# Layer 3 of a four-layer network: the short convolution moved from TensorE to VectorE and ScalarE, and one more state's product with C moved from VectorE to GpSimd

## The chip, the cores and the metric

The kernel runs on one core of one Trainium2 chip. The metric is device time in microseconds (us): the median of several executions of the whole program, of which layer 3 is the last part. A core has four engines that compute, each with its own queue of instructions, worked off in program order: TensorE (PE, matmuls into PSUM), VectorE (DVE), ScalarE (ACT) and GpSimd (POOL, which here reads and writes SBUF alone). SyncE (SP) issues DMAs. PEld is PE's loading of weights.

## The reference, cut to what matters

Four layers follow one another, each of the form x = x + f(groupnorm(x)), on two images of 192 channels and 96 x 96 positions. Layer 3, the one that the change touches, is a selective scan (a state-space layer) along the 9216 positions of each image:

```python
xz = x_flat @ W_in.T
x_in, z_gate = jnp.split(xz, 2, axis=-1)                  # 384 channels each
...
xc = lax.conv_general_dilated(xt_pad, conv_w, window_strides=(1,), padding='VALID',
                              feature_group_count=D_INNER) + conv_b[None, :, None]
x_conv = jax.nn.silu(xc)                                  # 4 taps per channel
x_dbl = jnp.einsum('bdl,kd->blk', x_conv, W_x)
dt, B_ssm, C_ssm = jnp.split(x_dbl, [DT_RANK, DT_RANK + D_STATE], axis=-1)
...
delta = jax.nn.softplus(dt_lin + b_dt)
def step(h, inp):                                         # 16 states per channel
    dA = jnp.exp(d_t[..., None] * A)
    h = dA * h + (d_t * u_t)[..., None] * B_t[:, None, :]
    y_t = jnp.einsum('bdn,bn->bd', h, C_t)
...
y = ys.transpose(1, 2, 0) + D[None, :, None] * x_conv
y = y * jax.nn.silu(z_gate.transpose(0, 2, 1))
out = jnp.einsum('bdl,cd->bcl', y, W_out)
```

The short convolution is causal: each of the 384 channels is a weighted sum of its value at a position and at the three before it, plus a bias.

## The kernel before, in words

Layer 3 (`layer3`, from L1730) works in 36 steps s: two images b of 18 chunks c, each of T = 512 positions. The 384 inner channels lie as ND = 3 blocks d of 128 partitions, so a full tile is 128 x 1536 in fp32. The state runs over NST = 16 states n, and a state of a chunk goes through this:

- `times_b` (L1902, POOL): bu = du times row n of B. B's row comes as bb, broadcast over the partitions by a DMA from DRAM (`load`, L1894, issued by SP). bu has three buffers, bb four.
- `decay` (L1907, ACT): da = exp(dl times A), into PSUM, one per d, three buffers.
- `scan` (L1916, DVE): h = scan of da and bu, three instructions, one per d. h has three buffers. `keep` (L1922, ACT) saves the last column as the state for the next chunk.
- the product with C. For most states, `spread` (L1926, PE) writes row n of C into PSUM as cc, by a matmul with 16 rows, into a single buffer, and `times_c` (L1937, DVE) forms hc = h times cc, with two buffers. For the states in the tuple `ASIDE` (L1738), C's row comes by DMA as ca, and `times_c` (L1932, POOL) forms hp = h times ca, into a single buffer, one state later.
- `sum_of` (L1945, PE): hc or hp is added into acc in PSUM by six matmul instructions with the identity; for the states in `ASIDE` two states after their product's turn.

Three generators bring the rest of the work, cut at their yields, so that a piece of each falls to each state:

- `output` (from L1957) for the step just ended: y = acc times zs (L1961, DVE), the matmuls with w_out (L1968, PE) and the addition of x (L1976, DVE).
- `late(s+1)` (from L1850), started at n = 3: the matmuls for B, C and dt (L1856), xd and its way to DRAM (br), the matmul for delta (L1871), and softplus: Abs, Relu, Exp, Identity on ACT (L1875 to L1878), at n = 8 a scalar_tensor_tensor on DVE (L1880) and Ln on ACT (L1881), at n = 9 three products on POOL (ln, dl, du: L1883 to L1885).
- `early(s+2)` (from L1800), started at n = 7: the normalised input xn (L1809, ACT), the projection (L1823, PE) in six pieces, copied out of PSUM by ACT to xi (L1831; the three last columns of the chunk before stand in front) and to zs (L1836), then the convolution: four matmuls per d with diagonal matrices, one per tap (L1840), and the bias on ACT on the way to us (L1844); then Silu of zs and us (L1846, L1847).

All three use one PSUM bank, pe, so a piece of PE's waits until the piece before it has been read. The diagonal matrices `taps` are made once (L1778, DVE).

The order on PE, ACT, DVE and POOL is the program's own, written out in the loop at the end of `layer3` (L1995 to L2031): for a state n, `spread`, `scan`, the sums that are due, `times_c` on DVE, `times_b` for two states on, `times_c` on POOL for the state before, the loads for four states on, `decay` for the next state, `keep`, then one piece each of `output`, `late` and `early`. Before the loop, early(0), late(0) and early(1) run through in one go (L1983).

Of the kernel before, what the change touches and what calls it, by code (L numbers as in the profile page):

```python
# [6 lines left out]
F32 = mybir.dt.float32  # L7
I32 = mybir.dt.int32
AF = mybir.ActivationFunctionType
ALU = mybir.AluOpType  # L10
# [8 lines left out]
P = 128  # L19
# [29 lines left out]
ND = DI // P  # L49
# [7 lines left out]
def halves(ap):  # L57

    return ap.rearrange("(k p) t -> p k t", k=2)


class Net:
# [1667 lines left out]
    def layer3(self, x, out, stats):  # L1730


        nc, tc, ins = self.nc, self.tc, self.ins
        T = 512
        NC = HW // T
        NBC = 2 * NST

        ASIDE = (1, 5, 9, 12)  # L1738
        gns = [self.gn(3, b, stats[b]) for b in range(B)]
        with ExitStack() as ctx:  # L1740
            wp = ctx.enter_context(tc.tile_pool(name="w3", bufs=1))
# [8 lines left out]
            cw = self.load("conv_w", [P, ND, 4], pool=wp)  # L1750
            cb = self.load("conv_b", [P, ND], pool=wp)
# [19 lines left out]
            dsk = self.load("D", [P, ND], pool=wp)  # L1771
            w_out = self.load("w_out", [P, ND, C], ins["w_out"].rearrange("(d p) o -> p d o", p=P), wp)

            taps = wp.tile([P, ND, 4, P], F32, name="taps")
            skip = wp.tile([P, ND, P], F32, name="skip")
            for d in range(ND):
                for j in range(4):
                    nc.vector.tensor_scalar(  # L1778
                        taps[:, d, j], self.ident, cw[:, d, j : j + 1], None, ALU.mult
                    )  # L1780
                nc.vector.tensor_scalar(skip[:, d], self.ident, dsk[:, d : d + 1], None, ALU.mult)
            state = wp.tile([P, NST, ND], F32, name="state")
            tail = wp.tile([P, ND, 3], F32, name="tail")
# [13 lines left out]
            def bank():  # L1797
                return ps.tile([P, T], F32, name="pe")

            def early(s):  # L1800


                b, c = steps[s]
                xt = sb.tile([CH, 2, T], F32, name="xt")
                nc.sync.dma_start(out=xt, in_=halves(x[b])[:, :, c * T : (c + 1) * T])
                xn = s1.tile([CH, 2, T], F32, name="xn")
                gs, gb = gns[b]
                for k in range(2):
                    nc.scalar.activation(  # L1809
                        xn[:, k], xt[:, k], AF.Identity, bias=gb[:, k : k + 1], scale=gs[:, k : k + 1]  # L1810
                    )
                us = sb.tile([P, ND, T], F32, name="us")
                zs = s3.tile([P, ND, T], F32, name="zs")
                xi = s1.tile([P, ND, T + 3], F32, name="xi")
                got[s] = {"us": us, "zs": zs}
                if c == 0:
                    nc.gpsimd.memset(tail, 0.0)
                nc.scalar.copy(xi[:, :, 0:3], tail)

                def project(at):  # L1820
                    pe = bank()
                    for k in range(2):
                        nc.tensor.matmul(  # L1823
                            pe, w_in[:, k, at : at + P], xn[:, k], start=k == 0, stop=k == 1
                        )
                    return pe

                for d in range(ND):
                    pe = project(d * P)
                    yield  # L1830
                    nc.scalar.copy(xi[:, d, 3:], pe)  # L1831
                nc.scalar.copy(tail, xi[:, :, T : T + 3])
                for d in range(ND):
                    pe = project(DI + d * P)
                    yield
                    nc.scalar.copy(zs[:, d], pe)  # L1836
                for d in range(ND):
                    pe = bank()
                    for j in range(4):
                        nc.tensor.matmul(  # L1840
                            pe, taps[:, d, j], xi[:, d, j : j + T], start=j == 0, stop=j == 3
                        )
                    yield
                    nc.scalar.activation(us[:, d], pe, AF.Identity, bias=cb[:, d : d + 1])  # L1844
                yield
                nc.scalar.activation(zs, zs, AF.Silu)  # L1846
                nc.scalar.activation(us, us, AF.Silu)  # L1847
                yield
# [39 lines left out]
            def load(s, n):  # L1888

                for name, row in (("bb", NST + n), ("ca", n))[: 1 + (n in ASIDE)]:  # L1890
                    t = sc.tile([P, T], F32, name=name) if name == "bb" else sb.tile(
# [32 lines left out]
            def spread(s, n):  # L1924
                cc = ps.tile([P, T], F32, name="cc")
                nc.tensor.matmul(cc, pick[:, n], got[s]["xd"][:NST], start=True, stop=True)  # L1926
                got[s]["cc", n] = cc

            def times_c(s, n):
                if n in ASIDE:  # L1930
                    hc = s1.tile([P, ND, T], F32, name="hp")
                    nc.gpsimd.tensor_tensor(  # L1932
                        hc, got[s]["h", n], over(got[s]["ca", n]), ALU.mult
                    )
                else:
                    hc = sb.tile([P, ND, T], F32, name="hc")
                    nc.vector.tensor_tensor(  # L1937
                        hc, got[s]["h", n], over(got[s]["cc", n]), ALU.mult
                    )
                got[s]["hc", n] = hc  # L1940

            def sum_of(s, n, last=False):
                hc = got[s]["hc", n]
                for d in range(ND):
                    nc.tensor.matmul(  # L1945
                        got[s]["acc"][:, d], self.ident, hc[:, d], start=False, stop=last
                    )
# [35 lines left out]
            for s, make in ((0, early), (0, late), (1, early)):  # L1983
                for _ in make(s):
                    pass
# [9 lines left out]
            for i, (s, n) in enumerate(chain):  # L1995
                if n == 3 and s + 1 < ns:
                    second = late(s + 1)
                if n == 7 and s + 2 < ns:
                    first = early(s + 2)
                if n not in ASIDE:  # L2000
                    spread(s, n)
# [9 lines left out]
                elif n > 1:  # L2011
                    if n - 1 not in ASIDE:
                        sum_of(s, n - 1)
                    if n - 3 in ASIDE:
                        sum_of(s, n - 3)
                if n not in ASIDE:
                    times_c(s, n)
# [110 lines left out]
```

## Time and profile before

| what | us |
|---|---|
| median of 3 runs | 11979.33 (11973.39 to 11980.73) |
| the profiled execution, its time | 11969.94 |
| the profiled execution, its span | 11968.2 |
| busy over the span: PE | 10378.3 (87%) |
| busy over the span: DVE | 8759.4 (73%) |
| busy over the span: POOL | 6998.9 (58%) |
| busy over the span: ACT | 6054.2 (51%) |
| mean granted clock of TensorE | 0.903 |

The profile is of one execution, and its lines name the engine, the line of the kernel, the operation, and output<-inputs by the program's names. "hc<-h,cc 128x1536 f32 x432 | 757.4, 1753 | 606.7 <-PE cc L1926 593.8" would be read: 432 instructions, 757.4 us busy in all, 1753 ns each on the average, and 606.7 us in which the engine stood idle just before them, of which 593.8 ended when PE had finished cc. In a timeline a line has its start and its length in us, and behind "x1" the idle time before it and what ended that. A matmul in fp32 shows as two instructions. The granted clock is the share of TensorE's clock that the chip let through.

### The profile page before, as it was taken

The numbers are of one execution on the slowest core, as the hardware profiler recorded it, in microseconds if no ns is written. First come the engines' busy times: TensorE is split into PE (matmuls) and PEld (weight loads), VectorE is DVE, ScalarE is ACT, GpSimd is POOL, SyncE is SP. The second block draws the span as 40 slices with busy tenths as digits, with TensorE's granted clock in tenths as the row PEclk, the third lists the DMA queues.
The fourth block names the chain that finished last, engine by engine and source line by source line (L and its number), as shares of the span: only waits on it lengthen the run. The fifth ranks groups of instructions, "written<-read, shape, count | busy, mean of one in ns | idle before, by whom it ended". The sixth has DMA issues, their size and how long they took to land. (4 is left out here: it accounts for less than half of the span.)

```text
span 11968.2 us, 226348 instructions
## 1 busy us (share of the span) xinstructions
PE 10378.3 (87%) x90181; PEld 6063.1 (51%) x90181; DVE 8759.4 (73%) x8880; ACT 6054.2 (51%) x11181; POOL 6998.9 (58%) x5569
## 2 busy tenths in 40 slices
PE   3599999999899999986767777769999999999998
PEld 2488888887788888872212222223333333333333
DVE  3777777776777777765688877747777777777778
ACT  0366666665666666750006533335555555555554
POOL 0366766765666666651036533327677767776777
PEclk9899999999999999998867777769899989988998
DMA  4534444433333333334323211112221222222121
GB/s 107 93 94 94 98 96 95 99 94 78 75 91 91 90 92 92 90 76 140 111 86 98 77 44 49 46 40 60 58 62 57 61 59 61 57 62 60 60 57 52
DMA packets 625509, 928.58 MB, mean 78 GB/s; under 512 B 240064, under 2 KB 325372, under 8 KB 623424
## 3 DMA queue, kind: packets, MB, share of 16 engines
q1 hardware_dynamic: 402248, 713.07, 22.4%
q0 software_dynamic: 103808, 133.18, 5.2%
q10 hardware_dynamic: 118392, 67.73, 1.9%
q8 instruction: 720, 11.80, 0.4%
q14 instruction: 341, 2.79, 0.1%
HBM read 475.14 MB, written 188.78 MB: 55 GB/s over the span
## 5 line engine op out<-in xcount | busy, mean ns | idle before, releaser
L1902 POOL TENSOR_TENSOR bu<-du,bb 128x1536 f32<-128x1536 f32 x576 | 1973.6, 3437 | 841.3 <-issue 538.0
L555 DVE TENSOR_TENSOR sp<-h 128x2304 f32<-128x2304 f32 x790 | 2168.0, 2776 | 20.5 <-ACT h L534 20.5
L1916 DVE TENSOR_TENSOR_SCAN h<-da,state,bu 128x512 f32<-128x512 f32 x1632 | 1962.8, 1263 | 67.3 <-ACT da L1907 45.9
L1907 ACT ACTIVATE da<-dl,sb_A_log 128x512 f32<-128x512 f32 x1728 | 1170.2, 689 | 1485.5 <-DVE h L1916 1479.7
L579 ACT COPY st<-pt 128x512 f32<-128x512 f32 (+1 forms) x2370 | 1219.0, 517 | 1308.7 <-PE pt L571 1239.7
L571 PE MATMUL pt<-ident,sp 128*128 128x128 f32 x14220 | 1680.0, 276 | 125.9 <-DVE sp L555 79.3
L577 DVE COPY st<-pt 128x512 f32<-128x512 f32 x1580 | 1061.3, 686 | 975.8 <-PE pt L571 959.8
L525 POOL TENSOR_TENSOR h<-u,step 128x1152 f32<-128x1152 f32 (+1 forms) x474 | 1201.4, 2547 | 816.6 <-DVE u L498 472.4
L571 PEld LDWEIGHTS pt<-ident,sp 128*128 128x128 f32 x14220 | 1566.7, 142 | 213.3 <-issue 90.1
L543 POOL DMA_DIRECT2D xw<-xp_d x2500 | 1391.7, 633 | 178.8 <-PE pt L618 82.6
L1945 PE MATMUL acc<-hc,ident 128*128 128x512 f32 x2592 | 1366.7, 668 | 8.5 <-DVE hc L1937 8.5
L1937 DVE TENSOR_TENSOR hc<-h,cc 128x1536 f32<-128x1536 f32 x432 | 757.4, 1753 | 606.7 <-PE cc L1926 593.8
L618 PE MATMUL pt<-st,xw 64*32 64x288 f32 (+1 forms) x30000 | 1070.9, 365 | 72.7 <-ACT st L579 27.9
L639 ACT COPY val<-pt 128x288 f32<-128x288 f32 (+1 forms) x3132 | 985.8, 398 | 205.2 <-PE pt L618 201.9
L686 PE MATMUL pf<-main,wd 126*64 126x128 f32 (+1 forms) x17064 | 962.1, 270 | 1.1 <-DMA main<-val 0.4
L686 PE MATMUL pf<-more,wl 54*64 54x128 f32 (+1 forms) x17064 | 953.2, 268 | 10.2 <-DMA more<-val 10.2
L686 PEld LDWEIGHTS pf<-main,wd 126*64 126x64 f32 x17064 | 889.6, 137 | 140.8 <-issue 138.5
L1945 PEld LDWEIGHTS acc<-hc,ident 128*128 128x128 f32 x2592 | 520.8, 212 | 857.3 <-issue 845.9
L686 PEld LDWEIGHTS pf<-more,wl 54*64 54x64 f32 x17064 | 916.1, 135 | 45.7 <-issue 32.0
L618 PEld LDWEIGHTS pt<-st,xw 64*32 64x32 f32 x30000 | 539.0, 106 | 477.0 <-ACT val L639 171.7
L1823 PE MATMUL pe<-xn,sb_w_in 96*128 96x512 f32 x864 | 499.2, 707 | 137.2 <-ACT xn L1809 91.4
L1926 PE MATMUL cc<-xd,pick 16*128 16x512 f32 x864 | 554.5, 725 | 23.0 <-DVE hc L1937 22.9
(317 smaller groups left out, 13751.3 us busy)
## 6 DMA issues: line engine op xcount, KB each, us to landing
main<-val SPq DMA_DIRECT2D x2016, 81.0 KB
bb<-br SPq DMA_DIRECT2D x576, 256.0 KB
more<-val SPq DMA_DIRECT2D x1728, 40.5 KB
xw<-xp_d POOLq DMA_DIRECT2D x2500, 26.0 KB
xt<-x_d SPq DMA_DIRECT2D x108, 384.0 KB
ca<-br SPq DMA_DIRECT2D x144, 256.0 KB
u_d<-u SPq DMA_DIRECT2D x158, 180.0 KB
raw<-o_d SPq DMA_DIRECT2D x156, 180.0 KB
```

The costliest lines, as they stand in the source:

```text
L525: nc.gpsimd.tensor_tensor(hs, u[:, :, 8 * KK * l : 8 * KK * l + n].unsqueeze(3).to_broadcast([P, 2, n, WS]), con["step"].unsqueeze(1).unsq ...
L543: nc.gpsimd.dma_start(out=xw[e * WN : (e + 1) * WN, i], in_=xp_d[y : y + WS, x : x + WS, e * CM // 2 : e * CM // 2 + XW],)
L555: nc.vector.tensor_tensor(sp.rearrange("p s (y x) -> p s y x", x=WS), hy.unsqueeze(3).to_broadcast([P, n, WS, WS]), hx.unsqueeze(2).to_bro ...
L571: nc.tensor.transpose(pt[:, q], sp[:, 2 * (q0 + q) : 2 * (q0 + q) + 2].rearrange("p e w -> p (e w)"), self.ident,)
L577: nc.vector.tensor_copy(st[:, q0 : q0 + m], pt[:, :m])
L579: nc.scalar.copy(st[:, q0 : q0 + m], pt[:, :m])
L618: nc.tensor.matmul(pvs[e][lane : lane + 32, j * w : (j + 1) * w], xw[e * WN : (e + 1) * WN, win, g * CG : g * CG + 32], sts[pair][e * WN : ...
L686: nc.tensor.matmul(to, wt[:, m * CO : (m + 1) * CO], took.rearrange("p h (r c) -> p h r c", c=columns), start=first and l == 0 and t == 0, ...
L1902: nc.gpsimd.tensor_tensor(bu, got[s]["du"], over(got[s]["bb", n]), ALU.mult)
L1907: nc.scalar.activation(da, got[s]["dl"][:, d], AF.Exp, scale=nA[:, d, n : n + 1])
L1916: nc.vector.tensor_tensor_scan(h[:, d], got[s]["da", n, d], bu[:, d], init, ALU.mult, ALU.add)
L1945: nc.tensor.matmul(got[s]["acc"][:, d], self.ident, hc[:, d], start=False, stop=last)
```

## The change

The convolution leaves PE. Its first tap becomes an ACT instruction that reads xi and writes us, with the tap's weight as scale and the bias; the other three become scalar_tensor_tensor instructions on DVE, us = xi times weight + us, in place, nine per step, issued next to the projection of zs. The matmuls with the diagonal matrices, their three yields, the bias on the way out of PSUM and the making of the matrices go. `early` has three pieces fewer, so Silu comes at an earlier state. And `ASIDE` has five states instead of four, three of them other ones.

```diff
-        ASIDE = (1, 5, 9, 12)
+        ASIDE = (1, 4, 7, 10, 12)
...
-            taps = wp.tile([P, ND, 4, P], F32, name="taps")
             skip = wp.tile([P, ND, P], F32, name="skip")
             for d in range(ND):
-                for j in range(4):
-                    nc.vector.tensor_scalar(
-                        taps[:, d, j], self.ident, cw[:, d, j : j + 1], None, ALU.mult
-                    )
                 nc.vector.tensor_scalar(skip[:, d], self.ident, dsk[:, d : d + 1], None, ALU.mult)
...
                     nc.scalar.copy(xi[:, d, 3:], pe)
+                    nc.scalar.activation(
+                        us[:, d], xi[:, d, :T], AF.Identity, bias=cb[:, d : d + 1], scale=cw[:, d, 0:1]
+                    )
                 nc.scalar.copy(tail, xi[:, :, T : T + 3])
                 for d in range(ND):
                     pe = project(DI + d * P)
+                    for j in range(1, 4):
+                        nc.vector.scalar_tensor_tensor(
+                            us[:, d], xi[:, d, j : j + T], cw[:, d, j : j + 1], us[:, d], ALU.mult, ALU.add
+                        )
                     yield
                     nc.scalar.copy(zs[:, d], pe)
-                for d in range(ND):
-                    pe = bank()
-                    for j in range(4):
-                        nc.tensor.matmul(
-                            pe, taps[:, d, j], xi[:, d, j : j + T], start=j == 0, stop=j == 3
-                        )
-                    yield
-                    nc.scalar.activation(us[:, d], pe, AF.Identity, bias=cb[:, d : d + 1])
                 yield
                 nc.scalar.activation(zs, zs, AF.Silu)
                 nc.scalar.activation(us, us, AF.Silu)
```

## The prediction

> **What bounds the kernel now.** I read the page, then parts of layer 3 alone: its waits, the timelines of DVE, POOL, PE and ACT over one step, and the granted clock by stretch. Layer 3 runs from about 8010 us to the end, in 36 steps. Its y (L1961), once in a step, in DVE's timeline (start, us, engine, line, wait before):
>
> ```profile
> 11662.24 1.76 DVE L1961 TENSOR_TENSOR y<-acc,zs 128x1536 f32<-128x1536 f32 x1 [7.30 <-PE acc L1945]
> 11771.46 1.76 DVE L1961 TENSOR_TENSOR y<-acc,zs 128x1536 f32<-128x1536 f32 x1 [7.31 <-PE acc L1945]
> 11869.93 1.76 DVE L1961 TENSOR_TENSOR y<-acc,zs 128x1536 f32<-128x1536 f32 x1 [3.44 <-PE acc L1945]
> ```
>
> A step takes 109.2 us; the third row ends a step without early. In one step (10121.8 to 10231.1) PE is busy 101.3, DVE 82.5, POOL 78.8, ACT 57.1. What DVE waits for between 8200 and 11800: us in all, times, longest:
>
> ```profile
> DVE hc L1937 <- PE cc L1926: 569.3, 264, 6.2
> DVE y L1961 <- PE acc L1945: 241.3, 33, 7.5
> ```
>
> So a step is 84.4 us of DVE's own (start to start: 16 triples of scans at 3.73, 12 hc at 1.67, y 1.68, L1880 1.67, two L1976 at 0.65) and about 25 us of waits, nearly all for PE. Three groups tell what is traded:
>
> ```profile
> L1902 POOL TENSOR_TENSOR bu<-du,bb 128x1536 f32<-128x1536 f32 x576 | 1973.6, 3437 | 841.3 <-issue 538.0
> L1916 DVE TENSOR_TENSOR_SCAN h<-da,state,bu 128x512 f32<-128x512 f32 x1632 | 1962.8, 1263 | 67.3 <-ACT da L1907 45.9
> L1937 DVE TENSOR_TENSOR hc<-h,cc 128x1536 f32<-128x1536 f32 x432 | 757.4, 1753 | 606.7 <-PE cc L1926 593.8
> ```
>
> The scans and hc have one input in PSUM (da, cc), and keep these times beside POOL. A DVE operation with both inputs in SBUF does not. Layer 1, DVE's timeline, then POOL's:
>
> ```profile
> 5959.47 1.74 DVE L1440 TENSOR_TENSOR t<-t,lr 96x1536 f32<-96x1536 f32 x1
> 5961.13 4.99 DVE L1434 TENSOR_TENSOR lr<-pad 96x1536 f32<-96x1536 f32 x1
> ```
>
> ```profile
> 5959.63 4.88 POOL L1431 TENSOR_TENSOR ud<-pad 96x1536 f32<-96x1536 f32 x1 [0.99 <-DVE pad L114]
> ```
>
> POOL issued while L1440 (both inputs in SBUF) ran; it took 4.88 instead of its shortest 3.45 and ended at 5964.51. L1434 issued as L1440 ended, but POOL was already waiting and went first; L1434 ended at 5966.12, one duration behind POOL. They exclude each other, and who waits goes next. In layer 3 it happens once, to the only such DVE operation there now (median 1.751):
>
> ```profile
> 11820.65 3.41 DVE L1880 SCALAR_TENSOR_TENSOR du<-ln,du 128x1536 f32<-128x1536 f32 x1
> ```
>
> ```profile
> 11819.00 3.44 POOL L1902 TENSOR_TENSOR bu<-du,bb 128x1536 f32<-128x1536 f32 x1 [1.96 <-issue]
> ```
>
> L1880 ends 1.62 us behind that product. The new taps read xi and us, both in SBUF.
>
> The clock in two stretches (length; PE, PEld, DVE, ACT, POOL busy; granted clock; DMA):
>
> ```profile
> 10060.00:10070.00 10.00, 8.76 (x12) 2.49 (x10) 9.35 (x8) 6.42 (x10) 8.18 (x3) 0.66 0.22 60
> 10070.00:10080.00 10.00, 8.69 (x10) 3.11 (x11) 3.80 (x3) 5.27 (x9) 3.43 (x1) 0.57 0.30 92
> ```
>
> Half clock follows thin work (matmuls of 16 and 44 rows) or a wait of 2 us, though PE is mostly busy.
>
> **The change, part by part (per step).**
> 1. PE loses the taps, three groups of eight L1840 at 3.55 us = 10.65, and one cc, 1.06: 11.7.
> 2. ACT loses three L1844 (0.68) and gains three scaled copies from SBUF; nearest row L1809, 0.80. They stand behind xi copies, and scan 10 needs the decays behind them only 5 us later: 0; without that cover 2.4.
> 3. DVE loses one hc (1.67) and gains nine scalar_tensor_tensor of 128x512. Nearest rows: L1687, the same operation, 0.67; L1719, with a pointer scalar, 0.74; start to start 0.61 to 0.67. I take 0.61, as for L1682 and L1683 back to back: 5.5 (at most 6.0). DVE's own work: 84.4 - 1.7 + 5.5 = 88.2.
> 4. POOL gains one hp, 24 operations at 3.4 = 81.6. Its ca goes through SP, which waits only for buffers: 0.
> 5. The generator is three yields shorter: Silu moves from n=1 to n=14, with the same two table loads. Scan 3 waited 0.8 for it; at n=14 an hc stands in between: 0 to -0.8, I take 0.
> 6. At the start, early(0) and early(1) run alone: 7967.74 to 7983.34 and 8037.85 to 8054.23 go, 32 us once. Their taps end while z is projected. The twelve L1778 (2.4 us) end before xi is there: 0.
>
> **The walk.** I followed the four queues through one step in program order with these durations; t=0 is the start of scan 0.
> - *y*: PE has no taps before the sum of state 15. The wait falls from 7.3 to the 3.4 of the third y row.
> - *n=1 to 7*: hc3 at 23.6 waits 1.8, hc5 at 36.4 waits 2.9 (before: 1.2, and hc6 2.5). Scan 7 ends at 47.
> - *hc8*: xn waits for ACT's Abs, Relu, Exp and Identity behind scan 7, then projection 0 (3.7 at half clock) and cc8 (2.07) pass on PE. Before: 11.4 from the end of scan 7 to hc8. The same now, but state 7 has no hc to fill it: DVE waits 7.7, not 6.
> - *hc9*: state 9 now has an hc. Its cc stands behind projection 1, which waits for the xi copy behind Ln (t=64). PE has no sums left for that gap and is at half clock: 3.7 + 2.07, hc9 at 69.9, a wait of 4.2 (before: hc10, 3.7).
>
> Waits: 3.4 + 1.8 + 2.9 + 7.7 + 4.2 = 20.0; without exclusion a step is 88.2 + 20.0 = 108.2. PE's relief of 11.7 buys little, since it was late for y alone; its other waits hang on chains through ACT. A check: the step between the second and third y row lacks all of early, 21.8 us of PE's work, and is only 10.7 shorter.
> - *The taps* stand at the ends of n=10, 11, 12, where POOL is fullest: ln, dl and du begin at 63.5 behind Ln, then bu12, bu13, hp10, bu14, bu15, hp12. Behind scan 10: tap, bu13 (3.4), tap, hp10 (3.4), tap: 6.8, and 2.0 more if bu12 still runs. Behind hc11 half of bu14 is left, 1.8, and bu15 isn't free before scan 12. Behind scan 12: tap, bu15, tap, hp12, tap: 6.9. Sum 15.5 (17.5 with bu12). The next scan is queued behind each waiting tap, and ACT's decays, PE's sums and POOL's next bu wait for that scan: nothing catches up. hp10 and hp12 share one buffer and each need a sum of PE first, which comes within 1 us of the turn; a late one drops its 3.4. I take one of two: 12.1.
>
> Step: 108.2 + 12.1 = 120.3, +11.1. Bounds of the exclusion: 0, if no tap meets a product, and 17.5. 34 of 36 steps have an early: 34 x 11.1 = 377, less 32: +345. The profiled execution (span 11968.2) took 11969.94, so 12315; the median of the runs is 9.4 above it, so 12325.
>
> **Two rules of the Trainium skill.** "GPSIMD Engine Reference", 1. Specifications, names "contention with DVE instructions in a 2-port perf mode or with two SBUF inputs". It speaks against this change and gives no price; the rows above show a whole turn waited. "TensorE: Matmul & The Clock Gate", Part 1, has PE throttled after an idle window of about 3.4 us; the first clock row differs, 0.66 with 8.76 of 10 us busy. By the page projection 0 and cc8 keep the full clock after a wait of 2 us, an estimate of 2.9 us less per step, 12226 in all; by the rows 12325.
>
> **Rivals.**
> - *The port does not bite* (faster): the taps slip between products. For it: only one of 36 L1880 was held. Against: L1880 comes while POOL waits for Ln, the taps while POOL is backed up. Step 108.2: 34 x -1.0 - 32 = -66, 11913. It decides if the waits for POOL sum to under 1.9 us per step.
> - *PE's relief passes whole* (faster): 109.2 - 11.7 = 97.5: 34 x -11.7 - 32 = -430, 11549. Against: the check above.
> - *A colder PE* (slower still): while DVE waits for POOL, PE idles, and sums 11 and 13 and a cc at half clock come into DVE's way: 2 x 2.66 + 1.06 = 6.4 more, 126.7: 34 x 17.5 - 32 = +563, 12542.
> - *Less exclusion* (slower, by less): both hp late, 116.9, and full clock through n=8, 114.0: 34 x 4.8 - 32 = +131, 12110.
>
> **Chances.** Forecast (116.9 to 125.7 a step: 12209 to 12508) 0.60; less exclusion 0.12; colder PE 0.10; within 0.2%, about what a measurement here can tell from no change, 0.05; the port does not bite 0.10; whole relief 0.03. So faster 0.13, same 0.05, slower 0.82. The range 12000 to 12560 holds the forecast, the lesser exclusion and most of the colder case.
>
> **What would show it.** Right: taps with a mean above 1.5 us, those of n=10 and 12 the longest; POOL's products above 3.44 in turn; y's wait about 3, hc9's about 4; steps of 120. Wrong: a tap mean near 0.7, or steps at or under 109, or the full clock through n=8.

## The result, and the profile after

The changed kernel takes 12298.48 us (median of 4 runs, 12292.43 to 12331.58) against 11976.36 (4 runs, 11968.79 to 11980.73) for the kernel before on the same chip: a ratio of 1.0271, 95% interval 1.0259 to 1.0282, or +322 us. The forecast was 12325, or +345.

The profiled execution of the changed kernel took 12331.58, its span 12329.5. Layer 3 sets in 33 us later in it than before (its L1767 starts at 7976.50 instead of 7943.19); that time arises in layers that the change does not touch, so the two traces are compared from there: 4353.0 us to the end instead of 4025.0, +328. Mean granted clock 0.877 instead of 0.903.

The taps as a group of the trace from 8000 us to the end (line, engine, operation, tiles; count; busy us, mean ns; idle before). They take nearly three times what such an instruction takes beside no product of POOL's (0.74, below):

```profile
L1834 DVE SCALAR_TENSOR_TENSOR us<-xi,sb_conv_w,us 128x512 f32<-128x512 f32 x315 | 679.1, 2156 | 15.0 <-ACT us L1827 7.6
```

What DVE waits for between 8200 and 11800, as shown for the kernel before (us, times, longest). This stretch holds 30 steps, and 33 of the kernel before. The wait of y has fallen from 7.3 a step to 1.8; that of hc has hardly changed, 17.0 a step (509.6 over 30) instead of 17.3 (569.3 over 33), but it lies at other states:

```profile
DVE hc L1931 <- PE cc L1920: 509.6, 151, 7.9
DVE y L1955 <- PE acc L1939: 53.7, 30, 4.8
DVE hc L1931 <- DVE h L1910: 1.4, 3, 0.5
```

One step on DVE, from hc8 to y (start, length, line; in brackets the wait). The three groups of taps stand behind scan 10, hc11 and scan 12:

```profile
10143.44 1.75 DVE L1931 TENSOR_TENSOR hc<-h,cc 128x1536 f32<-128x1536 f32 x1 [5.20 <-PE cc L1920]
10145.11 2.92 DVE L1874 SCALAR_TENSOR_TENSOR du<-ln,du 128x1536 f32<-128x1536 f32 x1
...
10155.89 1.75 DVE L1931 TENSOR_TENSOR hc<-h,cc 128x1536 f32<-128x1536 f32 x1 [4.32 <-PE cc L1920]
...
10161.11 10.58 DVE L1834 SCALAR_TENSOR_TENSOR us<-xi,sb_conv_w,us 128x512 f32<-128x512 f32 x3
...
10175.33 1.75 DVE L1931 TENSOR_TENSOR hc<-h,cc 128x1536 f32<-128x1536 f32 x1
10177.00 3.86 DVE L1834 SCALAR_TENSOR_TENSOR us<-xi,sb_conv_w,us 128x512 f32<-128x512 f32 x3
...
10184.33 5.34 DVE L1834 SCALAR_TENSOR_TENSOR us<-xi,sb_conv_w,us 128x512 f32<-128x512 f32 x3
...
10210.86 1.76 DVE L1955 TENSOR_TENSOR y<-acc,zs 128x1536 f32<-128x1536 f32 x1 [1.62 <-PE acc L1939]
```

POOL over the same stretch. The 10.58 lie beside bu12, bu13 and hp10: POOL's products and the taps end one after the other, in turn. In the second group only the first tap meets a product (bu14, until 10178.73); the two behind it, just as much in place, take 0.75 each. The last product of the fence, hp12, came only at 10195.03, when the third group was done, so that group met one product and not two:

```profile
10160.03 7.28 POOL L1896 TENSOR_TENSOR bu<-du,bb 128x1536 f32<-128x1536 f32 x2
10167.68 3.45 POOL L1926 TENSOR_TENSOR hp<-h,ca 128x1536 f32<-128x1536 f32 x1 [0.38 <-PE acc L1939]
10175.30 3.43 POOL L1896 TENSOR_TENSOR bu<-du,bb 128x1536 f32<-128x1536 f32 x1 [4.17 <-DVE h L1910]
10184.54 3.79 POOL L1896 TENSOR_TENSOR bu<-du,bb 128x1536 f32<-128x1536 f32 x1 [5.80 <-issue]
10195.03 3.44 POOL L1926 TENSOR_TENSOR hp<-h,ca 128x1536 f32<-128x1536 f32 x1 [6.70 <-issue]
```

From y to y a step takes 118.6 and 120.4 us in turn; the mean of the first 30 is 119.7, before 109.2.

### The profile page after: what moved, and what is told of

Its sections match the earlier page's. It is cut to its first block, busy times and chain, and to the rows that moved or that the text cites. A ratio compares the mean times of both kernels' runs of the same rounds, so it can differ in the third digit from the quotient of the medians.

```text
span 12329.5 us, 224855 instructions
## 1 busy us (share of the span) xinstructions
PE 10204.4 (83%) x89245; PEld 5965.6 (48%) x89245; DVE 9385.8 (76%) x9156; ACT 6075.8 (49%) x11181; POOL 7160.1 (58%) x5605
## 3 DMA queue, kind: packets, MB, share of 16 engines
q14 instruction: 343, 2.81, 0.1%
## 5 line engine op out<-in xcount | busy, mean ns | idle before, releaser
L1896 POOL TENSOR_TENSOR bu<-du,bb 128x1536 f32<-128x1536 f32 x576 | 2003.0, 3485 | 863.0 <-issue 433.9
L1939 PE MATMUL acc<-hc,ident 128*128 128x512 f32 x2376 | 1329.4, 704 | 10.7 <-DVE hc L1931 10.7
L1931 DVE TENSOR_TENSOR hc<-h,cc 128x1536 f32<-128x1536 f32 x396 | 694.4, 1754 | 609.5 <-PE cc L1920 589.0
L1818 PE MATMUL pe<-xn,sb_w_in 96*128 96x512 f32 x864 | 598.9, 830 | 569.8 <-ACT zs L1838 284.0
L686 PE MATMUL pf<-more,wl 54*64 54x128 f32 (+1 forms) x17064 | 957.2, 268 | 11.7 <-DMA more<-val 10.2
L1926 POOL TENSOR_TENSOR hp<-h,ca 128x1536 f32<-128x1536 f32 x180 | 624.7, 3470 | 257.2 <-issue 246.2
```

The costliest lines, as they stand in the source:

```text
L686: nc.tensor.matmul(to, wt[:, m * CO : (m + 1) * CO], took.rearrange("p h (r c) -> p h r c", c=columns), start=first and l == 0 and t == 0, ...
L1896: nc.gpsimd.tensor_tensor(bu, got[s]["du"], over(got[s]["bb", n]), ALU.mult)
L1939: nc.tensor.matmul(got[s]["acc"][:, d], self.ident, hc[:, d], start=False, stop=last)
```

## The experiments

Theory at the outset: the taps read SBUF twice and wait for POOL's products, whole turns at a time; that is the loss, since DVE is what a step hangs on. Rivals: the loss comes from the other choice of states, or from a PE that is late in new places.

All runs in one table. "Waits" are what DVE waited for cc and acc of PE, per step (30 steps from the first y on, from the profiled execution); "the rest" is the step less these waits, that is DVE's own work, the taps, their waits for POOL and what DVE waits for ACT's da and POOL's hp (1.9 before, none in the changed kernel). The ratios are to the kernel before as it ran beside each: 11976.36 for the changed kernel, 11980.84 for the next four rows, 11983.24 for the next four (five_with_9 to taps_psum_old_states), 11983.83 for the last four.

| kernel | median us | ratio to before (95%) | step | waits | rest |
|---|---|---|---|---|---|
| before | 11976.36 | 1 | 109.2 | 24.6 | 84.6 |
| after | 12298.48 | 1.0271 (1.0259-1.0282) | 119.7 | 18.7 | 100.9 |
| one_sbuf_input | 12066.25 | 1.0066 (1.0049-1.0083) | 112.7 | 24.4 | 88.3 |
| no_dve_taps | 11888.45 | 0.9923 (0.9907-0.9940) | 107.7 | 26.0 | 81.7 |
| conv_alone | 12439.37 | 1.0391 (1.0373-1.0408) | 123.8 | 16.8 | 107.1 |
| aside_alone | 12258.21 | 1.0232 (1.0215-1.0249) | 117.4 | 35.5 | 81.9 |
| five_with_9 | 12046.53 | 1.0060 (1.0044-1.0077) | 111.4 | 27.5 | 83.9 |
| one_sbuf_old_states | 11881.33 | 0.9919 (0.9902-0.9936) | 107.0 | 16.2 | 90.8 |
| relief_old_states | 11712.88 | 0.9778 (0.9761-0.9794) | 102.3 | 17.6 | 84.7 |
| taps_psum_old_states | 11872.81 | 0.9914 (0.9897-0.9930) | 106.4 | 14.8 | 91.6 |
| taps_psum_new_states | 11990.16 | 1.0009 (0.9998-1.0021) | 110.5 | 21.6 | 88.9 |
| taps_psum_five_with_9 | 11968.56 | 0.9985 (0.9972-0.9997) | 109.2 | 19.0 | 90.2 |
| after_with_9 | 12474.29 | 1.0416 (1.0393-1.0438) | 124.6 | 19.5 | 105.1 |
| taps_later | 12345.60 | 1.0301 (1.0279-1.0323) | 121.1 | 26.7 | 94.4 |

### The exclusion taken away

one_sbuf_input: the taps' second input is a decay tile in PSUM, so that no tap reads SBUF twice; the sum over the taps is left out by this. (18 of the 324 taps run before the first decay and keep us.)

```diff
-                            us[:, d], xi[:, d, j : j + T], cw[:, d, j : j + 1], us[:, d], ALU.mult, ALU.add
+                            us[:, d], xi[:, d, j : j + T], cw[:, d, j : j + 1],
+                            got["da"] if "da" in got else us[:, d], ALU.mult, ALU.add
...
                 got[s]["da", n, d] = da
+                if d == 0:
+                    got["da"] = da
```

> The nine taps of DVE keep their number, shape and place, but their second input is da, in PSUM, in place of us, so only one input is in SBUF; the sum over the taps is left out by this (us holds the last tap plus a da). Theory (a DVE operation with two SBUF inputs and a POOL product exclude each other): the taps fall from a mean of 2.16 us to 0.7, a step from 118.6 to about 104.4 (14.2 less), in all about 11816, below the kernel before. Rival (the taps cost what they cost as DVE work in a chain, whatever memory they read): taps stay above 1.5 us and the time between 12250 and 12330.

Measured 12066. The taps, from its groups of instructions:

```profile
L1834 DVE SCALAR_TENSOR_TENSOR us<-xi,sb_conv_w,da 128x512 f32<-128x512 f32 x306 | 226.9, 742 | 7.2
```

0.742 us instead of 2.156: the taps' waits for POOL are gone. The rest of a step falls by 100.9 - 88.3 = 12.6. The nine taps give back 12.8 of DVE's time; the scalar_tensor_tensor on du (L1874 in the changed kernel), which still reads SBUF twice, takes 2.81 on the average instead of 2.31, so this kernel is not wholly free of the exclusion. But a step falls by only 7.0, because the waits for PE rise by 5.7. Its DVE timeline shows where, at hc11, hc13 and hc14, none of which waits in the changed kernel:

```profile
10037.32 1.76 DVE L1934 TENSOR_TENSOR hc<-h,cc 128x1536 f32<-128x1536 f32 x1 [3.52 <-PE cc L1923]
10052.05 1.75 DVE L1934 TENSOR_TENSOR hc<-h,cc 128x1536 f32<-128x1536 f32 x1 [1.45 <-PE cc L1923]
10058.69 1.75 DVE L1934 TENSOR_TENSOR hc<-h,cc 128x1536 f32<-128x1536 f32 x1 [1.34 <-PE cc L1923]
```

So the exclusion holds, and my price for taking it away (11816) does not. In the changed kernel the taps' waits lie over a lateness of PE. The stretch table of the changed kernel (length; PE, PEld, DVE, ACT, POOL busy; clock; DMA) has the first group, 10042.43 to 10052.99, in it:

```profile
10040.00:10050.00 10.00, 10.00 (x24) 4.16 (x22) 9.93 (x6) 3.68 (x7) 10.00 (x4) 0.97 0.14 34
10050.00:10060.00 10.00, 3.38 (x6) 1.35 (x6) 9.90 (x6) 2.67 (x5) 5.83 (x2) 0.71 0.16 45
```

While DVE stands in the taps, PE works without a gap on what it owes, at clock 0.97: sums 9 and 7, projections 2 and 3, and cc11, done at 10051.3.

no_dve_taps: the nine taps on DVE are left out altogether.

```diff
-                    for j in range(1, 4):
-                        nc.vector.scalar_tensor_tensor(
-                            us[:, d], xi[:, d, j : j + T], cw[:, d, j : j + 1], us[:, d], ALU.mult, ALU.add
-                        )
```

> Taps 1 to 3 are left out: us is the first tap of ACT with the bias. It shows what is left of a step without any tap on DVE or PE. Theory: a step loses the 19.8 us that the three groups take, 98.8, in all about 11625; if another wait takes part of the room, 100 to 103, up to 11770. Rival (PE's relief was worth 11.7 a step by itself, the taps ate it): 97.5 a step, 11580. The distance to the run with one SBUF input is the taps' own work: 5.5 us a step, 190 in all, by the theory; some 20 us a step by the rival that prices them as DVE work.

Measured 11888. With no tap anywhere, and PE relieved of 11.7 us a step, a step is 107.7. What PE gave up comes back as waits for it (26.0, more than the 24.6 before the change); hc11 waits 6.00 and 5.21 in two successive steps. That the relief passes whole is refuted.

### The two halves alone

conv_alone is the changed kernel with the old states; aside_alone is the kernel before with the new ones.

```diff
-        ASIDE = (1, 4, 7, 10, 12)
+        ASIDE = (1, 5, 9, 12)
```

> The convolution as in the changed kernel, but the states by POOL as before (1, 5, 9, 12). Theory: the exclusion does it, so this is slower than before as well: one hc more on DVE (1.7), one product less on POOL, the taps behind hc10 and hc11 meet half a product each and more of the backlog behind ln: 113 to 119 a step, 12100 to 12310. Rival (the other choice of states does it, with hc9's wait and the empty slot on PE): 103 to 108 a step, under 11940.

```diff
-        ASIDE = (1, 5, 9, 12)
+        ASIDE = (1, 4, 7, 10, 12)
```

> The convolution on PE as before, the five states on POOL as in the change. Theory: DVE has one hc less, PE one cc less, POOL one product more; PE is late for y as before: 107 to 111 a step, 11900 to 12030, within 0.5% of before. Rival (the choice of states does it): 115 or more a step, over 12150.

Measured 12439 and 12258. The convolution alone costs +458 (against 11981 for the kernel before, run beside them), more than both together; the states alone +277, where I had expected a slight change: there my reading of the states fell, and the rival was right. Together they cost +322, not 735. (conv_alone lies 129 above what I had expected of it; why, the runs of the exclusion with the old states show.) In aside_alone the rest of a step is 2.7 shorter than before (one hc of 1.7 and 1.1 less of waits for da and hp make most of it), and the waits for PE are 10.9 longer. DVE's timeline there:

```profile
10009.98 1.75 DVE L1937 TENSOR_TENSOR hc<-h,cc 128x1536 f32<-128x1536 f32 x1 [7.85 <-PE cc L1926]
10021.26 1.75 DVE L1937 TENSOR_TENSOR hc<-h,cc 128x1536 f32<-128x1536 f32 x1 [4.32 <-PE cc L1926]
10035.50 1.75 DVE L1937 TENSOR_TENSOR hc<-h,cc 128x1536 f32<-128x1536 f32 x1 [5.41 <-PE cc L1926]
...
10072.36 1.76 DVE L1961 TENSOR_TENSOR y<-acc,zs 128x1536 f32<-128x1536 f32 x1 [7.31 <-PE acc L1945]
```

hc8 and hc11 now follow states without an hc, so DVE arrives earlier and waits; state 9 has an hc now, whose cc stands behind projection 1. PE, which still has the convolution, is no earlier. five_with_9 puts state 9 aside again, and keeps five:

```diff
-        ASIDE = (1, 5, 9, 12)
+        ASIDE = (1, 4, 6, 9, 12)
```

> The kernel before with five states by POOL, but 1, 4, 6, 9, 12: state 9 stays without an hc. With the five of the change (1, 4, 7, 10, 12) and the convolution on PE a step took about 116.5 instead of 109.2. Theory (it is the place: hc9 needs a cc that stands behind the projection which waits for the xi copy behind Ln, and PE then has no sums to do and goes to half clock): with state 9 free of cc the loss is gone, 107.5 to 110 a step, 11915 to 12010. Rival (it is the number: a fifth product on POOL delays bu and hp): 114 or more a step, over 12150.

Measured 12047, above what I expected by 37. So of the 277 it matters for 212 which the five states are (7 and 10, or 6 and 9); what is left, +66, goes with a fifth state on POOL, and with 4 and 6 in the place of 5. One cost of these states is L1880, the scalar_tensor_tensor on du, which reads SBUF twice: it takes 1.80 on the average before, 2.33 in aside_alone and 3.50 in five_with_9, because POOL is then at a product when it comes:

```profile
10004.34 3.23 DVE L1880 SCALAR_TENSOR_TENSOR du<-ln,du 128x1536 f32<-128x1536 f32 x1
```

```profile
10002.52 3.43 POOL L1902 TENSOR_TENSOR bu<-du,bb 128x1536 f32<-128x1536 f32 x1
```

The +1.7 a step in five_with_9 is not far below the 2.2 that its step is longer than before; but hc10 waits 7.2 for PE behind it, which can hide it, and no run shows what it is worth.

### The exclusion with the old states

The edits of one_sbuf_input and no_dve_taps, with the old states.

> The taps on DVE with one input in SBUF (da from PSUM in place of us; the sum over the taps is left out), and the states by POOL as before (1, 5, 9, 12). With both inputs in SBUF this choice of states took 124 a step, 23.3 of it in the taps. Theory: exclusion is 17.7 of the 23.3, less what PE takes of the room: 107 to 112 a step, 11900 to 12070. Rival (with these states the taps wait for something else): over 118 a step, 12280.

> Taps 1 to 3 are left out, and the states by POOL as before: PE's relief of the convolution alone. Theory (PE was late for y alone, the other waits hang on chains through ACT): y's wait falls from 7.3 to 2 or 3 and little else: 103.5 to 105.5 a step, 11740 to 11820. Rival (the relief passes whole): 98.6 a step, 11585.

Measured 11881 and 11713, 19 and 27 below what the theory gave. Against conv_alone the exclusion costs 558 us with these states, 123.8 - 107.0 = 16.8 a step; seen from DVE it is 107.06 - 90.84 = 16.2 and the waits for PE stay nearly as they are (16.8 and 16.2). Here next to nothing is hidden. The difference lies ahead of the taps. conv_alone on DVE, from hc10:

```profile
10075.32 1.75 DVE L1931 TENSOR_TENSOR hc<-h,cc 128x1536 f32<-128x1536 f32 x1 [2.39 <-PE cc L1920]
10076.99 11.01 DVE L1834 SCALAR_TENSOR_TENSOR us<-xi,sb_conv_w,us 128x512 f32<-128x512 f32 x3
...
10093.32 3.86 DVE L1834 SCALAR_TENSOR_TENSOR us<-xi,sb_conv_w,us 128x512 f32<-128x512 f32 x3
...
10100.64 8.39 DVE L1834 SCALAR_TENSOR_TENSOR us<-xi,sb_conv_w,us 128x512 f32<-128x512 f32 x3
```

State 10 has an hc there, which first waits for PE; then the taps wait for POOL; the two waits stand one behind the other. With the new states the taps come before the next hc that needs PE, and one wait runs inside the other. The third group is also longer here, 8.39, since hp12 isn't late. relief_old_states bears out that PE was late for y above all: without taps on either engine a step is 6.9 shorter than before, the waits for y fall from 7.3 to 1.6, and those for hc by 1.2.

### Is it the hiding? State 9 put aside, and the taps moved

after_with_9 is the changed kernel with states that are better by 212 where the convolution is on PE, and in which state 10 has an hc in front of the taps.

```diff
-        ASIDE = (1, 4, 7, 10, 12)
+        ASIDE = (1, 4, 6, 9, 12)
```

> The changed kernel with the states (1, 4, 6, 9, 12), its taps reading SBUF twice. Theory: the exclusion and the lateness of PE at hc9 and hc11 hide one another; with state 9 aside there is less lateness to hide it, so the exclusion costs nearly its whole (12 to 16 us per step, as with the old states): 12300 to 12450, steps of 119 to 124, not faster than the changed kernel's 12298 although its states are the better ones by 212 without the taps on DVE. Rival, that the two add up: 12298 - 212, so 12050 to 12130, steps of about 113.

taps_later moves the taps away from POOL's fullest stretch.

```diff
                     pe = project(DI + d * P)
+                    yield
+                    nc.scalar.copy(zs[:, d], pe)
+                for d in range(ND):
                     for j in range(1, 4):
...
                     yield
-                    nc.scalar.copy(zs[:, d], pe)
```

> The changed kernel with its nine taps moved behind the projection of z, from n = 10 to 12 to n = 13 to 15; they still read SBUF twice. Theory: a group waits for the products that POOL has in its queue just there; behind n = 12 only one bu per state and one hp are left, so each group meets one product instead of up to two: groups of about 5.5 + 5.5 + 3.9 = 15 instead of 19.8, and a step of 112 to 117: 12040 to 12220. Rival, that the place does not matter because each tap waits for a product wherever it stands: 12250 to 12350.

after_with_9 came to 12474: the better states make the changed kernel slower by 176 us. This is the direction that the hiding foresaw, 24 us beyond its upper end; that the parts add up (12050 to 12130) is refuted. No run takes the exclusion away with these states and the taps in this place, so its price here is not measured by itself. Its DVE timeline has the wait for PE in front of the group, as in conv_alone:

```profile
10093.65 1.75 DVE L1931 TENSOR_TENSOR hc<-h,cc 128x1536 f32<-128x1536 f32 x1 [5.93 <-PE cc L1920]
10095.33 9.12 DVE L1834 SCALAR_TENSOR_TENSOR us<-xi,sb_conv_w,us 128x512 f32<-128x512 f32 x3
```

taps_later came to 12346, and my theory's time (12040 to 12220) fell, though the groups did what it said: 2.32 + 8.06 + 3.91 = 14.3 us, expected 15. The rest of a step fell by 6.5, and the waits for PE rose by 8.0:

```profile
10038.56 1.75 DVE L1933 TENSOR_TENSOR hc<-h,cc 128x1536 f32<-128x1536 f32 x1 [4.32 <-PE cc L1922]
...
10053.33 1.75 DVE L1933 TENSOR_TENSOR hc<-h,cc 128x1536 f32<-128x1536 f32 x1 [5.95 <-PE cc L1922]
...
10065.56 1.75 DVE L1933 TENSOR_TENSOR hc<-h,cc 128x1536 f32<-128x1536 f32 x1 [3.41 <-PE cc L1922]
10067.24 2.32 DVE L1837 SCALAR_TENSOR_TENSOR us<-xi,sb_conv_w,us 128x512 f32<-128x512 f32 x3
```

Between hc9 and hc11 DVE has nothing but scans now, and waits 5.95 for cc11; the taps then stand where PE is not late. The rival's number was right for another reason than it gave: a tap does meet fewer products at the later place, but at the earlier place some 6 us of the wait were free. (This reading came after the run; no forecast of it was made.)

### The sum over the taps in PSUM

Here the convolution is whole: the first tap goes to the PSUM bank that the projections use, the next two add to it there, and the last writes us, in three pieces behind the projection of z. No tap reads SBUF twice; the scalar_tensor_tensor on du still does.

```diff
-                    nc.scalar.activation(
-                        us[:, d], xi[:, d, :T], AF.Identity, bias=cb[:, d : d + 1], scale=cw[:, d, 0:1]
-                    )
                 nc.scalar.copy(tail, xi[:, :, T : T + 3])
                 for d in range(ND):
                     pe = project(DI + d * P)
+                    yield
+                    nc.scalar.copy(zs[:, d], pe)
+                for d in range(ND):
+                    pe = bank()
+                    nc.scalar.activation(
+                        pe, xi[:, d, :T], AF.Identity, bias=cb[:, d : d + 1], scale=cw[:, d, 0:1]
+                    )
+                    yield
                     for j in range(1, 4):
                         nc.vector.scalar_tensor_tensor(
-                            us[:, d], xi[:, d, j : j + T], cw[:, d, j : j + 1], us[:, d], ALU.mult, ALU.add
-                        )
-                    yield
-                    nc.scalar.copy(zs[:, d], pe)
+                            us[:, d] if j == 3 else pe, xi[:, d, j : j + T], cw[:, d, j : j + 1], pe,
+                            ALU.mult, ALU.add,
+                        )
```

With the old states, the changed kernel's, and (1, 4, 6, 9, 12):

> The whole convolution, on ACT and DVE, with its sum held in the PSUM bank pe between the taps, so that every tap has one input in SBUF and one in PSUM; in three pieces behind the z projections (n = 13 to 15, and DVE's last at n = 0), states by POOL as before. Theory (exclusion): taps at 0.75 each, 6.7 a step beside 104.5 without them, DVE has some slack there: 105 to 111 a step, 11800 to 12030. Rival (the taps' place on DVE ahead of the scans costs, whatever they read): 115 or more, over 12180.

> The whole convolution with the sum over the taps held in a PSUM bank, in three pieces behind the projection of z, with the states of the changed kernel (1, 4, 7, 10, 12). Theory: with the exclusion gone, what is left of the slowdown is the choice of states, as in the run with one SBUF input at 12066; the three later pieces changed that by -9 with the old states (11881 to 11873). So 12000 to 12120, steps of 111 to 114, taps of about 0.74 us. Rival, that the states cost by themselves what they cost with the convolution on PE (+277 on 11873): 12120 to 12180.

> The same with the states (1, 4, 6, 9, 12): five aside, state 9 among them. Theory: the states' loss is the place of hc9, whose cc stands behind projection 1; with it gone, 212 as between the two runs with the convolution on PE (12258 to 12047), or somewhat less because PE has room now: 11850 to 11950. Rival, that hc9's place matters only while PE has the taps: within 60 of the run with the changed kernel's states, 12000 to 12120.

With the old states it takes 11873, 0.9% less than the kernel before and 3.5% less than the changed one. A tap takes 0.75, as in the groups of that run:

```profile
L1839 DVE SCALAR_TENSOR_TENSOR pe<-xi,sb_conv_w,pe 128x512 f32<-128x512 f32 x216 | 162.7, 753 | 62.1 <-ACT pe L1834 58.3
```

With the changed kernel's states 11990, 10 below the range that I gave, and no different from before (0.9998 to 1.0021). With state 9 put aside as well 11969, where I had expected 11850 to 11950: 22 us better and not some 200, so the place of hc9 is worth little once PE has no taps, as the rival had it, whose range it misses by 31. Four states beat five wherever no tap reads SBUF twice: on PE (11976 and 12047 or 12258), with one SBUF input (11881 and 12066), without taps (11713 and 11888) and in PSUM. Part of it can be du's turn with POOL, whose operation takes 1.80 with the old states, 2.55 with the changed kernel's and 3.25 with the last; this is not shown by itself.

## Why the prediction was right

The sum came out within 27 us. Taken term by term it describes the changed kernel for the reasons given; but the prediction built it as a step without exclusion, 108.2, and a price of exclusion on top, 12.1, and there the runs show 112.7 (with the 1.1 that du still waits for POOL) and 7.0. The two errors, 4.5 too little and 5.1 too much, cancel in the total; that much of its closeness is luck, and it decides what a repair is worth.

- **DVE's own work**, 88.2: the run whose taps wait for no product has 88.3. Three errors cancel there. A tap takes 0.74 and not 0.61 from start to start (+1.1). L1874 meets a product of POOL's there (2.80 and not 1.67 from start to start, +1.1); the prediction left out that the new states bring this about (2.33 in aside_alone, where they alone differ). And the 48 scans take 57.7 from start to start and not 16 x 3.73 = 59.7 (-2.0); before the change it was 58.0 already.
- **The taps' waits for POOL**, 12.1: measured 12.8 on the mean of 30 steps. By the groups of the step shown, less 2.2 for three taps alone: 8.4 at n=10, 1.6 at n=11, 3.1 at n=12, foreseen 6.8, 1.8 and 3.5 (with one late hp, which is hp12). At n=10 bu12 did still run, the 2.0 that the text had kept for its upper end.
- **The waits for PE**, 20.0: measured 18.7. y 1.8 (3.4 foreseen), hc3 2.1 (1.8), hc5 3.5 (2.9), hc8 5.2 and 7.9 in turn (7.7), hc9 4.3 (4.2), hc2 0.4 (none). y was the largest miss: the row it was taken from ends a step without early, and why the others wait less is open. The agreement is with the changed kernel; without the taps' waits PE is waited for 24.4 a step, and the walk had none of the 6.3 at hc11, hc13 and hc14.
- **The step**, 120.3: 119.7; and 32 once: the first scan starts 85.5 us after L1767, before 117.3, so 31.8.
- **"without exclusion a step is 108.2"** and "nothing catches up": this failed. The run whose taps wait for no product has 112.7. The prediction took the waits for PE and for POOL one after another; in the changed kernel PE works off 10 us of arrears while DVE stands in the first group, so 5.7 of the 12.6 are paid anyway. "Nothing catches up" is right with the old states (16.2 of 16.8), where the hc of state 10 waits before the taps do.
- **The colder PE**, a rival by which PE idles while DVE waits for POOL: no. It was busy 10.00 of 10 us at clock 0.97, and hc11 and hc13 wait for nothing.
- **PE's relief**: "it was late for y alone" is borne out in the main by relief_old_states, at 5.7 a step for y, where 3.9 was foreseen, and 1.2 for all hc.
- **The choice of states** was walked through for hc8 and hc9 (7.7 and 4.2) but not asked by itself. It costs 277 with the convolution on PE, 117 with the taps in PSUM, and gains 141 with the taps in SBUF.

Of the two rules of the Trainium skill, that of "GPSIMD Engine Reference", 1. Specifications, was borne out: two SBUF inputs on DVE contend with POOL, and the price here is a whole turn, 12.8 to 16.2 us a step for nine taps. "TensorE: Matmul & The Clock Gate", Part 1, has the clock throttled after an idle window of about 3.4 us; the prediction took from it that a wait of 2 us leaves the clock alone. The trace differs: projection 0 took 3.78 behind a wait of 2.53, and 1.98 in the next step, behind a wait of 0.90:

```profile
10020.11 3.78 PE L1818 MATMUL pe<-xn,sb_w_in 96*128 96x512 f32 x4 [2.53 <-ACT xn L1804]
10140.37 1.98 PE L1818 MATMUL pe<-xn,sb_w_in 96*128 96x512 f32 x4 [0.90 <-ACT xn L1804]
```

The stretch table shows how (as above): the clock went to half at 10020.10, at the end of a stretch of 3.41 us in which PE was busy for 0.89:

```profile
10016.69:10020.10 3.41, 0.89 (x3) 0.06 (x1) 1.30 (x2) 3.38 (x4) 3.41 (x2) 1.00 0.25 49
10020.10:10040.58 20.48, 14.96 (x16) 4.86 (x17) 10.33 (x8) 11.73 (x18) 14.19 (x5) 0.50 0.19 50
```

Where projection 0 ran fast hc8 waited 5.20 instead of 7.95, 2.75 less and close to the 2.9 that was estimated by the page; but L1874 then came while POOL was at work and took 2.92 instead of 1.75. So the two kinds of step differ by 1.8, not 2.75.

What stays open: how much of the lateness of PE at hc8, hc9 and hc11 is the half clock and how much the order of the work. Projection 1 takes 3.78 and cc9 2.07 behind a wait of 5.5 for xi, and no run changed the clock alone. Open too is how far the clock sets the steps. The clock record of every run changes in layer 3 only at whole multiples of 3.413 us from one change to the next, and in twelve of the fourteen kernels most steps repeat, singly or two to five together, after a whole number of these: 109.23 us before is 32, 112.64 in one_sbuf_input 33, 102.37 in relief_old_states 30, and 238.93 for two steps of the changed kernel 70. That a step falls into this grid is a reading of these sums and not tested. If it holds, part of a small saving can be lost or a small loss grow in settling there, so a difference of 1 or 2 us a step between two runs is not the price of one instruction.

## What to carry to other kernels

An engine's wait is worth what the step loses without it, not its length: the same taps cost 16.8 us a step where a wait for PE stood ahead of them, and 7.0 where their wait ran beside PE's arrears. A VectorE operation that is put next to a busy GpSimd should have one of its inputs in PSUM: here, with the old states and the taps placed later, that turned +3.9% into -0.9%, and the change of the operand alone into -0.8%. Two edits in one change are to be run apart, each with the other in both places, since here either made the step's states better or worse according to the other.

## What the runs showed of the hardware

- A VectorE operation with two SBUF inputs and a GpSimd product take turns of whole instructions. It holds for the 128x1536 L1874 too: 2.31 us on the average over 36 (1.75 alone), and 3.61 in after_with_9, at most 4.10. Scans and products with one input in PSUM kept their times (means of 1.261 to 1.264, and of 1.753 to 1.754, in all fourteen runs).
- A kernel can settle in steps that differ in turn (118.6 and 120.4; 105.2 and 109.9 in no_dve_taps), with projection 0 at half clock in one kind and not in the other. A walk through one step can't find this; the mean lies 0.9 us from either kind here.
